# Edge scores by columns sorted on the sign of W2, with self loops as items

## The chip, the cores and the metric

The kernel runs on one core of a Trainium2 chip. The metric is device time in microseconds (us); lower is better. Three runs of the kernel before took 2976.23, 2982.51 and 2991.17 us; the median is 2982.51.

## What is computed

Four graph layers run over 32 batch entries of 512 nodes with 256 features; adj is 512 x 512 and sparse. Layers 0 and 3 are of the kind that this change touches:

```python
pre_u = jnp.einsum('bud,dk->buk', h_t, W1[:d])
pre_v = jnp.einsum('bvd,dk->bvk', h_t, W1[d:])
hidden = jax.nn.relu(pre_u[:, :, None, :] + pre_v[:, None, :, :] + b1)
S = jax.nn.sigmoid(jnp.einsum('buvk,ko->buvo', hidden, W2)[..., 0] + b2[0])
a_t = jnp.einsum('buv,bud->bvd', S * A_a, h_t)
m_t = jnp.einsum('uv,bud->bvd', A_m, h_t) * h_t
z_t = beta1 * h_t + beta2 * (jnp.einsum('bvd,de->bve', a_t, Wa) + ba) \
    + beta3 * (jnp.einsum('bvd,de->bve', m_t, Wm) + bm)
```

Layer 1 is z + relu(adj z W' + b). Layer 2 is a softmax attention whose logits are leaky_relu(f1[i] + f1[j]) + adj. For S the sum over k of relu(pre_u + pre_v + b1) W2 is needed only where adj is not zero, since S is multiplied by adj.

## The kernel before

**Groups and passes.** The batch is worked in eight groups of four entries (NB = 4). For each group and each of layers 0 and 3 there is one pass over the edges, so 16 passes.

**Tables.** `first` (layer 0) and the end of `middle_one` (layer 3) call `pre`. For each entry and each of four chunks of 128 nodes, two matmuls (L592, L594) give pre_u and pre_v; VectorE adds b1 to pre_u (L596), ScalarE copies pre_v (L597), and a DMA on SyncE's queue (SP) writes both as rows to a table in DRAM (L604). Three `puv` buffers take turns. For the self loops `pre` also forms relu(pre_u + b1 + pre_v) (L599) and sums it with W2 into `self_s` (L600).

**Items.** `Edges` holds the edges as 36 items of 128 edges: for each chunk of 128 nodes eight items with one edge a node, and four panels for nodes with more edges. In `edges`, `fetch` loads the pre_u rows of a chunk once as `mine` (L692, SP queue) and for each item gathers pre_v rows by an indirect DMA on GpSimd's queue (POOL). For each item VectorE adds `mine` to `rows` (L731, 1024 elements a partition: four entries by 256 columns). Then one of two ways follows. Every other item has one wide multiply, relu(rows) * W2 (L739), and ScalarE sums the four parts of 256 by activations with an accumulator (L717); the other items have four multiplies of 256 with an accumulator on VectorE (L747). In the first and the last pass (`spare` buffers) ScalarE sums all items. After each four items come an exponential on ScalarE (L614), the rest of the sigmoid on VectorE (L618, L619, L675), and indirect DMAs that put the results into `cells` in DRAM (L639). The self loops have their own sigmoid and two small DMAs to the diagonal (`own_1`).

**The middle stage.** `middle_one` reads `cells` back as SA and runs the rest of layer 0, then layers 1 and 2, and the tables of layer 3, one entry after the other. Its softmax passes between ScalarE (L958, L962), VectorE (L959 to L964) and TensorE transposes (L1003) several times. `last` and, for the last group, `last_before` and `last_behind` do the rest of layer 3 and write the output.

**Order.** `weave` merges these generators by due times given as fractions of a group's middle stage: while group t is in its middle stage, the tables and edges of layer 0 of group t + 1 and the edges and the end of layer 3 of group t - 1 run. `behind` adds an order without a wait, so that an edge operation is not set ahead of the middle stage's last marked operation on that engine. Each engine works its queue in order. The first 245 us hold the preparation: loads, the edge lists (`build`), the tables of groups 0 and 1, and the first edge pass, before the middle stage's own matmuls begin at L891.

Of the kernel before, what the change touches and what calls it, by code (L numbers as in the profile page):

```python
# [16 lines left out]
P = 128  # L17
# [17 lines left out]
EARLY = 20  # L35
CELLS = HALF * N
ITEMS = NC * OWN + 2 * PANELS
SPARE = NC // 2 * OWN * P + LINES
GROUP = NB * D
HELD = 12  # L40

# [7 lines left out]
class Model:  # L49


    def __init__(self, ctx, tc, a):
# [6 lines left out]
        for c in range(NC):  # L59
            nc.sync.dma_start(self.adj[:, c, :], a["adj"][c * P : (c + 1) * P, :])  # L60
        self.g0, self.g3 = self.gnn_first("L0_gnn"), self.gnn_first("L3_gnn")
# [36 lines left out]
    def gnn_first(self, L):  # L98
        nc, a, const = self.nc, self.a, self.const
        w = {"L": L}  # L100
        w["W1"] = self.load(f"{L}_W1", [P, 2 * DC, D], a[f"{L}_W1"].rearrange("(c p) k -> p c k", p=P))
        w["b1bc"] = self.bcast(f"{L}_b1", D)
        w["W2bc"] = const.tile([P, D], F32, name=f"{L}_W2bc")
        nc.scalar.dma_start(w["W2bc"], a[f"{L}_W2"].rearrange("k o -> (k o)").partition_broadcast(P))
        w["b2"] = self.bcast(f"{L}_b2", 1)
        w["nb2"] = const.tile([P, 1], F32, name=f"{L}_nb2")
        w["bcol"] = const.tile([P, DC, 1], F32, name=f"{L}_bcol")
        if L == "L3_gnn":
            w["bbc"] = const.tile([P, D], F32, name=f"{L}_bbc")
# [67 lines left out]
class Counts:  # L177
# [3 lines left out]
    def __init__(self, ctx, m):  # L181
# [4 lines left out]
        with tc.tile_pool(name="c_sb", bufs=2) as sb, tc.tile_pool(name="c_ps", bufs=1, space=PSUM) as ps:  # L186
            ones = sb.tile([P, N], F32, name="c_ones", bufs=1)
            nc.vector.memset(ones, 1.0)
            count = sb.tile([P, NC], F32, name="count", bufs=1)
# [17 lines left out]
            nc.vector.tensor_reduce(half, pc.rearrange("p (h c) -> p h c", h=2), AX.X, ALU.add)  # L207
            most = sb.tile([1, 1], F32, name="most")
            nc.vector.tensor_reduce(most, half, AX.X, ALU.max)
            nc.vector.tensor_scalar(self.excess, most, float(-LINES), None, ALU.add)  # L210
# [193 lines left out]
class Group:  # L404
# [3 lines left out]
    def __init__(self, sp, w, name):  # L408
# [7 lines left out]
        self.self_s = sp.grp.tile([P, NC, NB], F32, name=f"self_s{name[0]}")  # L416

# [5 lines left out]
class Sparse:  # L423
# [3 lines left out]
    def __init__(self, ctx, m, counts, xr, outr, B):  # L427
# [16 lines left out]
        self.act, self.small, self.gath = pool("act", 1), pool("small", 2), pool("gath", 5)  # L444
# [78 lines left out]
    def big(self, dtype, n, layer=None):  # L523

        self.bigs += 1
        if layer is None:
            layer = 3 if self.bigs <= NC else 0
        return self.act.tile([P, n], dtype, name="big", tag=f"SA{layer}", bufs=NC)

    def setup(self):  # L530


        for w in (self.m.g0, self.m.g3):
            self.nc.vector.tensor_scalar(w["nb2"], w["b2"], -1.0, None, ALU.mult)
        self.zero = self.act.tile([P, GROUP], F32, name="zero", tag="hWa3")
# [30 lines left out]
    def setup_rest(self):  # L566
        yield from self.rest

# [13 lines left out]
    def pre(self, g, b, hT):  # L582
# [3 lines left out]
        for c in range(NC):  # L586
            cs = slice(c * P, (c + 1) * P)
            if c % 2 == 0:
# [7 lines left out]
            nc.vector.tensor_tensor(puv[:, 0, :], pp[:, 0:D], w["b1bc"], ALU.add)  # L596
            nc.scalar.copy(puv[:, 1, :], pp[:, D:])  # L597
            both = self.small.tile([P, D], F32, name="both", bufs=1)
            nc.vector.tensor_tensor(both, pp[:, D:], puv[:, 0, :], ALU.add)  # L599
            nc.vector.scalar_tensor_tensor(  # L600
                both, both, 0.0, w["W2bc"], ALU.max, ALU.mult, accum_out=g.self_s[:, c, b : b + 1]
            )
# [47 lines left out]
    def edges(self, g, spare=(), own_tags=()):  # L650
# [8 lines left out]
        tags = [None] * 5 + list(spare)  # L659
# [3 lines left out]
        def own_1():  # L663
            self.sigmoid_of(own)
            diag = self.counts.diag.unsqueeze(2).to_broadcast([P, NC, NB])
            nc.vector.tensor_tensor(g.self_s, g.self_s, diag, ALU.mult)
            for q in range(2):
                diagonal = g.cells[q][q * HALF : q * HALF + HALF * (N + 1), :]
                diagonal = diagonal.rearrange("(c p a) b -> p c a b", p=P, a=N + 1)[:, :, 0, :]
                self.written(g, q, nc.sync.dma_start(diagonal, g.self_s[:, 2 * q : 2 * q + 2, :]))  # L670
# [9 lines left out]
        panels = [j for j in e.order if j >= NC * OWN][: len(own_tags)]  # L680

        def fetch(n):
# [4 lines left out]
            j = e.order[n]  # L687
            c = -j if -j in mine and j >= NC * OWN else j // OWN
# [13 lines left out]
            self.fetch(rows, g, e.iv[:, j : j + 1])  # L702
# [10 lines left out]
        def sums(k, rows):  # L713
# [13 lines left out]
        for k in range(ITEMS):  # L727
# [4 lines left out]
            if k + lead < ITEMS:  # L732
                fetch(k + lead)
# [716 lines left out]
```

## Time and profile before

| | us |
|---|---|
| median of three runs | 2982.51 |
| profiled execution | 2998.45 |
| its span on the core | 2996.8 |

The profiler recorded one execution. Engines are PE (TensorE matmul), PEld (weight load), DVE (VectorE), ACT (ScalarE), POOL (GpSimd) and SP (SyncE). A row of a group gives the line, engine and operation, output and input with their sizes, the count, then the busy time in us and the mean of one in ns, then the idle time of the engine just before them and what ended it. A row of the waits gives who waited for whom, the sum in us, how often and the longest. "issue" is time in which the profile shows no wait. The timeline gives start and duration in us.

The page lists the busy share of PE in 40 slices of 75 us, in tenths: the first eight are 6, 3, 6, 7, 7, 8, 7, 9 and later ones mostly 8 or 9.

### The profile page before, as it was taken

What the parts mean: (1) busy time and instruction counts of PE and PEld (TensorE: products, weight loads), DVE (VectorE), ACT (ScalarE), POOL (GpSimd) and SP (SyncE); (2) the same over time, 40 slices, a digit from 0 to 9 for tenths busy, and PEclk for the clock granted to TensorE, in tenths of its full rate; (3) what the DMA queues carried; (4) which work ended last, traced back from release to release, by engine and by line L of the source; (5) the groups of instructions that cost most, each with busy time, mean ns of one, the idle gap of its engine ahead of it and who ended that gap; (6) DMA issues with size and microseconds to landing.
All of it is one profiled execution on the core that took longest, in us unless ns stands there. A gap on an engine that the chain in (4) does not pass through costs nothing. (4 is left out here: it accounts for less than half of the span.)

```text
span 2996.8 us, 32453 instructions
## 1 busy us (share of the span) xinstructions
PE 2690.0 (90%) x8645; PEld 1613.9 (54%) x8646; DVE 2307.1 (77%) x6035; ACT 1336.8 (45%) x4101; POOL 1555.3 (52%) x1328
## 2 busy tenths in 40 slices
PE   6367787989998999989999899989999899988998
PEld 3134344545664566546664466646565466644666
DVE  6874786889588885988778885888858896783494
ACT  3553454445344443544344443445434453453262
POOL 2662463646445673556536464466735564361183
PEclk9678998999999999999999999999999999999999
DMA  8875657796678867787677866687677866663474
GB/s 268 286 225 169 213 174 221 233 300 203 217 217 269 268 211 227 230 262 254 209 222 247 275 207 230 216 268 253 211 228 236 303 227 197 208 211 102 148 244 150
DMA packets 302143, 677.30 MB, mean 226 GB/s; under 512 B 52608, under 2 KB 170880, under 8 KB 293760
## 3 DMA queue, kind: packets, MB, share of 16 engines
q0 software_dynamic: 122688, 414.40, 42.9%
q1 hardware_dynamic: 160304, 223.52, 23.0%
q10 hardware_dynamic: 18960, 37.24, 3.4%
q8 instruction: 70, 1.15, 0.2%
q14 instruction: 121, 0.99, 0.1%
HBM read 529.02 MB, written 146.01 MB: 225 GB/s over the span
## 5 line engine op out<-in xcount | busy, mean ns | idle before, releaser
L646 POOL DMA_INDIRECT rows<-table,iv x552 | 679.0, 1230 | 795.5 <-DMA table<-puv 262.7
L639 POOL DMA_INDIRECT cells<-s,cell x576 | 697.6, 1211 | 420.6 <-DVE s L675 243.2
L731 DVE TENSOR_TENSOR rows<-rows,mine 128x1024 f32<-128x1024 f32 x552 | 666.4, 1215 | 101.4 <-DMA rows<-table,iv 72.8
L717 ACT ACTIVATE rows<-rows 128x256 f32<-128x256 f32 x1088 | 439.6, 406 | 445.4 <-DVE rows L739 396.6
L46 PE MATMUL pst<-adj,h 128*128 128x512 f32 x1024 | 452.2, 592 | 0.0
L747 DVE SCALAR_TENSOR_TENSOR rows<-rows,L_gnn_W2bc 128x256 f32<-128x256 f32 x1120 | 414.0, 417 | 1.6
L739 DVE SCALAR_TENSOR_TENSOR rows<-rows,L_gnn_W2bc 128x1024 f32<-128x1024 f32 x272 | 329.4, 1213 | 0.4
L46 PEld LDWEIGHTS pst<-adj,h 128*128 128x128 f32 x1024 | 192.8, 190 | 219.9 <-issue 217.6
L46 PE MATMUL pst<-L_gnn_Wa,hT 128*128 128x256 f32 x1024 | 248.8, 393 | 62.9 <-DMA hT<-xT 57.8
L46 PEld LDWEIGHTS pst<-L_gnn_Wa,hT 128*128 128x128 f32 x1024 | 198.9, 199 | 103.0 <-issue 59.2
L46 PE MATMUL pst<-eT,feats 128*128 128x512 f32 x512 | 237.7, 619 | 10.9 <-ACT eT L1004 10.9
L46 PE MATMUL pst<-adjT,zW 128*128 128x512 f32 x512 | 228.2, 599 | 11.6 <-ACT zW L916 9.7
L596 DVE TENSOR_TENSOR puv<-pst,bc_L_gnn_b 128x256 f32<-128x256 f32 x256 | 104.9, 416 | 162.4 <-DMA table<-puv 89.2
L597 ACT COPY puv<-pst 128x256 f32<-128x256 f32 x256 | 93.2, 371 | 288.1 <-DVE puv L596 225.9
L1061 PE MATMUL pst<-hWa,SA 128*128 128x256 f32 x896 | 220.3, 400 | 0.0
L1061 PEld LDWEIGHTS pst<-hWa,SA 128*128 128x128 f32 x896 | 213.8, 328 | 3.7 <-issue 1.7
L717 ACT ACTIVATION_READ_ACCUMULATOR rows<-rows 128x1 f32 x1088 | 204.7, 188 | 0.0
L860 ACT COPY flat<-SA 128x512 f32<-128x512 f32 x128 | 136.7, 1128 | 136.6 <-issue 62.9
L891 PE MATMUL pst<-flat,hWa 128*128 128x512 f32 x448 | 196.8, 592 | 0.0
L592 PE MATMUL pst<-w_L_gnn_W,hT 128*128 128x512 f32 x256 | 141.5, 681 | 53.9 <-ACT hT L579 36.5
L46 PEld LDWEIGHTS pst<-eT,feats 128*128 128x128 f32 x512 | 99.9, 198 | 133.2 <-issue 113.3
L46 PEld LDWEIGHTS pst<-adjT,zW 128*128 128x128 f32 x512 | 96.5, 191 | 133.4 <-issue 114.0
(176 smaller groups left out, 3984.2 us busy)
## 6 DMA issues: line engine op xcount, KB each, us to landing
table<-puv SPq DMA_DIRECT2D x256, 256.0 KB
SA<-cells POOLq DMA_DIRECT2D x64, 1024.0 KB
h<-in_x_dram SPq DMA_DIRECT2D x64, 512.0 KB
mine<-table SPq DMA_DIRECT2D x64, 512.0 KB
hT<-xT SPq DMA_DIRECT2D x36, 512.0 KB
xT<-hT ACTq DMA_DIRECT2D x32, 512.0 KB
x2T<-yT SPq DMA_DIRECT2D x32, 512.0 KB
x2s<-x ACTq DMA_DIRECT2D x64, 256.0 KB
```

What stands on the lines that cost most here:

```text
L46: nc.tensor.matmul(out, lhsT, rhs, start=(n == 0), stop=(n == len(pairs) - 1))
L592: nc.tensor.matmul(pp, hT[:, 0, ks], w["W1"][:, 0::DC, :], start=True, stop=False)
L596: nc.vector.tensor_tensor(puv[:, 0, :], pp[:, 0:D], w["b1bc"], ALU.add)
L639: ins = self.nc.gpsimd.indirect_dma_start(out=g.cells[half], out_offset=bass.IndirectOffsetOnAxis(ap=at, axis=0), in_=s, in_offset=None)
L646: self.nc.gpsimd.indirect_dma_start(out=rows, out_offset=None, in_=g.table, in_offset=bass.IndirectOffsetOnAxis(ap=at, axis=0))
L717: self.behind(nc.scalar.activation(part, part, AF.Identity, accum_out=g.s[:, k, b : b + 1]))
L731: self.behind(nc.vector.tensor_tensor(rows, rows, other, ALU.add))
L739: nc.vector.scalar_tensor_tensor(by_entry, by_entry, 0.0, w2, ALU.max, ALU.mult)
L747: nc.vector.scalar_tensor_tensor(part, part, 0.0, w["W2bc"], ALU.max, ALU.mult, accum_out=at)
L860: self.nc.scalar.copy(flat[:, r, :], SA[r][:, :, b])
L891: nc.tensor.matmul(pz, hWa[:, r, cs], flat[:, r, :], start=(r == 0), stop=False)
L1061: self.nc.tensor.matmul(pz[:, k * D : (k + 1) * D], SA[r][:, cs, b], hWa[:, r, :], start=(r + k == 0), stop=(alone and k == 1 and r == NC ...
```

## The change

- `Counts` gets `ranks`: for each of layers 0 and 3 it counts the positive entries of W2 and gives every column a place: 112 columns (SURE) with positive W2 first, then 112 with negative W2, then the remaining 32 (MIXED). The branch to the dense path is also taken if fewer than 112 columns have one of the signs. W2 and b1 are loaded as columns, not as broadcast rows.
- `sorted_W1` reorders the columns of W1, b1 and W2 with one-hot matrices on TensorE, and scales each of the first 224 columns: pre_u's by -W2 and pre_v's by W2 (su = 1 + sure (-W2 - 1), sv = 1 + sure (W2 - 1)). It runs once for layer 0 in `setup` and once for layer 3 in `setup_rest`. The tables then hold -W2 (pre_u + b1) and W2 pre_v.
- With that, W2 relu(u + v) is max(W2 v, -W2 u) + W2 u for a positive W2 and min(W2 v, -W2 u) + W2 u for a negative one. An item takes a max over 4 x 112 columns, a min over 4 x 112, an add over 4 x 32, and the old multiply over 4 x 32 only. The sum of W2 u over the sure columns depends on the node alone: `pre` forms it with an accumulator (`less`) and it is subtracted from the item's sums; for panels it is subtracted in the rows, over 4 x 224.
- Of every four items ScalarE sums three; VectorE sums the fourth by one reduction over 1024. Self loops become four more items (40 steps a pass): their pre_v rows are loaded by a plain DMA on SP's queue, and ScalarE sums them. `pre` loses the two operations for the self loops.
- `max`, `min` and `add` are set behind the middle stage; before, the add was. The row tiles go from five to six, EARLY from 20 to 24.

```diff
-EARLY = 20
+EARLY = 24
+STEPS = ITEMS + NC
+SURE = 112
+MIXED = D - 2 * SURE
+PLACE = {0: 0, 2: 1, 1: 2, 3: 3}
...
+    def ranks(self, m, sb, ps, ones):
...
+        nc.vector.tensor_scalar(pos, w2, 0.0, None, ALU.is_gt)
+        pb = ps.tile([P, DC, 2], F32, name="c_pb")
+        mm(nc, pb[:, 0, :], [(before, pos[:, 0, :])])
+        mm(nc, pb[:, 1, :], [(before, pos[:, 1, :]), (ones[:, 0:P], pos[:, 0, :])])
+        pn = ps.tile([1, 2], F32, name="c_pn")
+        mm(nc, pn, [(ones[:, 0:1], pos[:, c, :]) for c in range(DC)])
...
+        nc.vector.tensor_scalar(far, rank, float(SURE), float(SURE), ALU.is_ge, ALU.mult)
+        nc.vector.tensor_tensor(place, rank, far, ALU.add)
+        nc.vector.tensor_scalar(far, rank, float(D - SURE), float(SURE - D), ALU.is_ge, ALU.mult)
+        nc.vector.tensor_tensor(place, place, far, ALU.add)
...
+    def sorted_W1(self, w):
...
+        for to, scale in ((by_u, w["su"]), (by_v, w["sv"])):
+            for c in range(DC):
+                nc.vector.tensor_scalar(
+                    to[:, c, :], self.m.upto_D, w["place"][:, c, :], scale[:, c, :], ALU.is_equal, ALU.mult
+                )
+        for c in range(DC):
+            pt = self.psum()
+            for r in range(2 * DC):
+                nc.tensor.transpose(pt[:, r * P : (r + 1) * P], w["W1"][:, r, c * P : (c + 1) * P], self.m.ident)
+            nc.scalar.copy(W1T[:, c, :], pt)
+        for k, to in enumerate((by_u, by_v)):
+            pp = self.psum()
+            for d in range(DC):
+                rs = slice((DC * k + d) * P, (DC * k + d + 1) * P)
+                mm(nc, pp[:, d * D : (d + 1) * D], [(W1T[:, c, rs], to[:, c, :]) for c in range(DC)])
+            nc.scalar.copy(w["W1"][:, DC * k : DC * (k + 1), :], by_two(pp))
...
     def pre(self, g, b, hT):
...
-            nc.vector.tensor_tensor(puv[:, 0, :], pp[:, 0:D], w["b1bc"], ALU.add)
+            nc.vector.scalar_tensor_tensor(
+                puv[:, 0, sure], pp[:, sure], 1.0, w["b1bc"][:, sure], ALU.mult, ALU.add, accum_out=less
+            )
+            nc.vector.tensor_tensor(puv[:, 0, 2 * SURE :], pp[:, 2 * SURE : D], w["b1bc"][:, 2 * SURE :], ALU.add)
             nc.scalar.copy(puv[:, 1, :], pp[:, D:])
-            both = self.small.tile([P, D], F32, name="both", bufs=1)
-            nc.vector.tensor_tensor(both, pp[:, D:], puv[:, 0, :], ALU.add)
-            nc.vector.scalar_tensor_tensor(
-                both, both, 0.0, w["W2bc"], ALU.max, ALU.mult, accum_out=g.self_s[:, c, b : b + 1]
-            )
...
     def edges(self, g, spare=(), own_tags=()):
...
-            self.fetch(rows, g, e.iv[:, j : j + 1])
+            if k < 0:
+                nc.sync.dma_start(rows, places[c, 1])
+            else:
+                self.fetch(rows, g, e.iv[:, j : j + 1])
...
-        todo = [(2, lambda: self.exp_of(w, own)), (4, own_1)]
+        w2 = w["W2bc"].unsqueeze(1).to_broadcast([P, NB, MIXED])
+        todo = [(last_own + 3, own_less), (last_own + 4, own_1)]
...
-            self.behind(nc.vector.tensor_tensor(rows, rows, other, ALU.add))
+            self.behind(nc.vector.tensor_tensor(rows[:, :, ups], rows[:, :, ups], other[:, :, ups], ALU.max))
...
-            if spare or k % 2 == 1 and k < ITEMS - 3:
-                by_entry = rows.rearrange("p (b d) -> p b d", b=NB)
-                w2 = w["W2bc"].unsqueeze(1).to_broadcast([P, NB, D])
-                nc.vector.scalar_tensor_tensor(by_entry, by_entry, 0.0, w2, ALU.max, ALU.mult)
-                summed.append(lambda k=k, rows=rows: sums(k, rows))
+            for cols, op in ((downs, ALU.min), (mixed, ALU.add)):
+                self.behind(nc.vector.tensor_tensor(rows[:, :, cols], rows[:, :, cols], other[:, :, cols], op))
+            nc.vector.scalar_tensor_tensor(rows[:, :, mixed], rows[:, :, mixed], 0.0, w2, ALU.max, ALU.mult)
+            if k >= 0 and e.order[k] >= NC * OWN:
+                sure = slice(0, 2 * SURE)
+                nc.vector.tensor_tensor(rows[:, :, sure], rows[:, :, sure], other[:, :, sure], ALU.subtract)
+            to = g.s[:, k, :] if k >= 0 else g.self_s[:, PLACE[-1 - k], :]
+            if spare or k < 0 or k % 4 and k < ITEMS - 3:
+                line = rows.rearrange("p b d -> p (b d)")
+                summed.append(lambda to=to, line=line: sums(to, line))
                 if spare:
                     summed.pop(0)()
             else:
-                for b in range(NB):
-                    part = rows[:, b * D : (b + 1) * D]
-                    at = g.s[:, k, b : b + 1]
-                    nc.vector.scalar_tensor_tensor(part, part, 0.0, w["W2bc"], ALU.max, ALU.mult, accum_out=at)
+                nc.vector.tensor_reduce(to, rows, AX.X, ALU.add)
...
-    step = (b - a) / ITEMS
+    step = (b - a) / STEPS
```

## The prediction

> **What bounds the kernel now.** The engine sums come first, then the stages, then what ends TensorE's waits in them.
>
> ```profile
> span 2996.8 us, 32453 instructions
> ...
> PE 2690.0 (90%) x8645; PEld 1613.9 (54%) x8646; DVE 2307.1 (77%) x6035; ACT 1336.8 (45%) x4101; POOL 1555.3 (52%) x1328
> ```
>
> TensorE (PE) is the bound, and the change takes nothing from its work. Time can come only out of its 307 us of idle time (2996.8 - 2690.0). The question is where those are. The windows view, cut by stage, has for each stretch the busy time of PE, its weight loads, VectorE (DVE), ScalarE (ACT) and GpSimd (POOL), then the granted TensorE clock, the DMA share and GB/s:
>
> ```profile
> 0.00:90.00 90.00, 57.53 (x193) 31.36 (x194) 54.01 (x199) 32.87 (x84) 26.19 (x44) 0.92 0.85 280
> 90.00:250.00 160.00, 81.30 (x202) 43.87 (x202) 121.60 (x240) 83.92 (x345) 102.35 (x82) 0.73 0.76 251
> 250.00:650.00 400.00, 334.32 (x976) 178.16 (x977) 301.75 (x827) 189.21 (x526) 189.49 (x165) 0.91 0.64 207
> 650.00:2650.00 2000.00, 1906.03 (x6232) 1150.38 (x6230) 1621.83 (x4364) 892.68 (x2674) 1095.39 (x919) 0.99 0.73 235
> 2650.00:2800.00 150.00, 133.02 (x420) 78.64 (x421) 81.89 (x229) 64.41 (x153) 41.93 (x40) 0.94 0.37 121
> 2800.00:2997.00 197.00, 177.76 (x626) 131.53 (x624) 126.03 (x178) 73.72 (x320) 99.96 (x80) 0.96 0.61 203
> ```
>
> PE idles 32, 79, 66, 94, 17 and 19 us in them. So half the idle time lies in the first 650 us. The waits of PE over the whole run, longest first:
>
> ```profile
> PE pst L46 <- DMA hT<-xT: 57.8, 4, 25.7
> PE pst L1003 <- DVE ex L964: 51.7, 27, 10.8
> PE pst L592 <- ACT hT L579: 36.5, 11, 4.9
> PE pst L1003 <- DVE cols L963: 29.3, 8, 6.3
> ```
>
> L1003 is the transposes of the softmax; DVE is late there because it works in order and edge items stand before the softmax. Adding the waits view up stage by stage, waits that DVE ended are 47.2 us in 250 to 650, 58.4 in 650 to 2650 and 22.1 after; those that ACT ended 14.5, 34.1 and 1.5. In 90 to 250 PE waits 57.8 us for hT<-xT: that load needs the buffer which L801, in DVE's queue, still reads.
>
> **The work on DVE.** The groups of the edge stage and of the stage that writes the tables:
>
> ```profile
> L731 DVE TENSOR_TENSOR rows<-rows,mine 128x1024 f32<-128x1024 f32 x552 | 666.4, 1215 | 101.4 <-DMA rows<-table,iv 72.8
> L717 ACT ACTIVATE rows<-rows 128x256 f32<-128x256 f32 x1088 | 439.6, 406 | 445.4 <-DVE rows L739 396.6
> L747 DVE SCALAR_TENSOR_TENSOR rows<-rows,L_gnn_W2bc 128x256 f32<-128x256 f32 x1120 | 414.0, 417 | 1.6
> L739 DVE SCALAR_TENSOR_TENSOR rows<-rows,L_gnn_W2bc 128x1024 f32<-128x1024 f32 x272 | 329.4, 1213 | 0.4
> ```
>
> The means overlap: the timeline of VectorE gives the distance from start to start.
>
> ```profile
> 1401.54 2.35 DVE L731 TENSOR_TENSOR rows<-rows,mine 128x1024 f32<-128x1024 f32 x2
> 1403.82 1.21 DVE L739 SCALAR_TENSOR_TENSOR rows<-rows,L_gnn_W2bc 128x1024 f32<-128x1024 f32 x1
> 1404.95 0.41 DVE L747 SCALAR_TENSOR_TENSOR rows<-rows,L_gnn_W2bc 128x256 f32<-128x256 f32 x1
> 1405.29 0.08 DVE L747 DVE_READ_ACCUMULATOR rows<-rows,L_gnn_W2bc 128x1 f32 x1
> ```
>
> Two operations of 1024 take 2.28 us, one takes 1.14, one of 256 takes 0.345. A line through both is 0.08 us plus 1.035 ns an element: 0.544 for 448 (4x112), 0.212 for 128 (4x32), 1.007 for 896, 0.312 for 224, 0.113 for 32. No row has the strided 4x112 form or max and min; I price them by this line.
>
> Before, over 16 passes of 36 items: 576 adds at 1.14 = 657 us; 296 wide multiplies at 1.14 = 337; 1120 narrow ones at 0.345 = 386; and 768 operations of 256 in `pre` at 0.345 = 265. Together 1645 us.
>
> After, with 40 items a pass, 640 in all: max and min of 448, add and multiply of 128, 1.512 us an item = 968. The 168 items that DVE still sums take one reduction of 1024 each: 168 x 1.14 = 192. The 64 panel items take a subtraction of 896: 64. `pre`: 256 x (0.312 + 0.113) = 109. Subtracting `less`, about 160 operations of 16 elements at 0.09 (neighbour: L618): 14. Together 1347. **DVE loses 298 us**, 18.6 a pass.
>
> [...]
>
> **The work on ACT.** Items summed there go from 296 to 472: 704 more activations. In the timeline ACT starts one every 0.40 us with its accumulator read, so +282 us, 45% to 54% of the span. [...] The rows agree on price, 4 x 0.40 = 1.60 us an item on ACT against 1.14 for a reduction on DVE: 176 items cost 81 us of engine time more. [...] I decide by whose queue PE waits for: DVE is 81% busy in the long stage, ACT 45%.
>
> **Stage by stage, against the 2998.45 us of the profiled execution.**
>
> 0 to 90: **+1**. Ahead of the branch some 20 small operations join the chain behind the last mask (neighbours 0.08 to 0.20 us apart): +3. Behind it the first layer's sort is 8 transposes, 12 matmuls and 4 ACT copies of 0.58, before the first matmul with W1 at 24.8; h arrives at 21, so about 2 of it shows. `pre` of the first group gives back 16 x 0.61 = 9.8 on DVE, of which I credit 4, as DVE waits 12.5 there for table<-puv. Bounds -3 to +8. The second layer's sort, PE work of some 4 us, falls where PE idles.
>
> 90 to 250: **-15**. DVE is packed from 90 to 182. 36 x 2.28 becomes 40 x 1.51 + 4 x 1.01: -17.6; `pre` of the second group -9.8; second sort +2. Of these 25 I credit 60%, as DVE also waited 38 us here. ACT's four more items (6.4 us) fit into its 76 idle us. Bounds 0 and -25.
>
> 650 to 2650: **-19**. ACT sums 744 / 4 = 186 items here, so some 11.6 passes: DVE -216, from 81% to 70% busy. If waiting behind other work goes with busy over idle, 4.3 becomes 2.4: 45% off the 58.4 us, -26. ACT goes to 56% by the same count (139 items x 1.60 = 223); that alone would add 56% to its 34.1 us, +19. But ACT is held up too: "ACT rows L717 <- DVE rows L739" is 299 us here and ACT's five longest waits for DVE make 624; shorter ones there give the 223 back. Between 0 and +19 I take +7. Bounds -50 and +25.
>
> 250 to 650: **-18**: 45% of 47.2 less 3 for ACT. No clock gain is credited. Bounds -45 and +10.
>
> 2650 to the end: **-9**, 45% of 22.1 less 1. The last pass sums all on ACT, 64 us instead of 58, beside DVE's 36 x 2.28 = 82 that becomes 65; the 28 us of L1061 behind the SA loads stay. Bounds 0 and -20.
>
> **Costed at nothing.** POOL keeps its 576 row fetches and 576 puts. The 64 loads of own rows, 512 KB each, go into SP's queue in order, where each waits for one of six row buffers; behind it stand table<-puv, h, hT and x2T. SP's mine loads, the nearest case, wait 6.6 us each ("SPq L692 <- DVE rows L731: 146.0, 22, 16.3"), yet after 650 PE waits only 0.8 us for any load in the long stage. If that slack is gone, 64 x 6.6 us of queue time is what can leak. The diagonal's sigmoid moves from step 4 to about step 28 of 40; its two small writes still stand ahead of the last puts.
>
> **Sum**: 1 - 15 - 18 - 19 - 9 = -60: 2998.45 becomes 2938. The median of the runs, 2982.51, is 0.9947 of the profiled execution; so **2923 us**.
>
> **Rivals.**
> 1. *ACT takes DVE's place, slower.* Place: the middle stage's copies (hT, zW, eT), queued in order behind a sum that waits for DVE. For it: 115 of the 186 summed items waited, 2.6 us each. If waits do not shorten, 326 items give 202 waits, 525 us blocked, and ACT is (893 + 624 + 223 + 226) / 2000 = 98% taken. One more such wait on the path in each of 32 batch entries is +83 us, against the gains of 60: 3021, by the median 3005. It decides from 60 / 32 = 1.9 us an entry. Against it: an item's DVE part falls from 2.28 to 1.51 us.
> 2. *Transfers hide the gain.* In 650 to 2650 DVE waits 64.7 us for table<-puv and 46.4 for rows, with DMA at 0.73, and 64 x 512 KB = 33.6 MB come on top of 677 MB. Then only start and end gain: 1 - 15 - 9, and about +5 for the transfers: -18, 2980, by the median 2965. Against it: PE's DVE waits end mostly with softmax operations.
> 3. *More is freed.* Idle between 90 and 2800 falls by nearly half (-120) as stalls chain, and the clock of 0.91 before 650 recovers: 2878, by the median 2863.
> 4. The branch could choose the dense path if a sign count left 112 to 144; both layers' W2 have 133 positive of 256. Nothing is reserved for it.
>
> **Chances**: forecast 0.50, rival 1 0.17, rival 2 0.20, rival 3 0.13. A measurement here tells 0.5% from no change, 2967.6 to 2997.4. Faster: nearly all of the forecast and of rival 3 and under half of rival 2, 0.70; same 0.15; slower 0.15. The range 2850 to 2988 leaves out most of rival 1 and the low end of rival 3.
>
> **What would show it.** Right: DVE near 2010 us, ACT near 1620, POOL unchanged; the waits on L964 and L963 halved; the first softmax transposes before 272 us instead of 282. Wrong: waits of PE on ACT copies over 100 us (rival 1); DVE's waits on rows and table<-puv grown by what its work lost (rival 2); 4x112 operations over 0.62 us apart.

## The result, and the profile after

Four runs of the changed kernel took 3020.24 to 3036.07 us, median **3031.07**; four of the kernel before 2976.23 to 2991.17, median 2985.21. The ratio is **1.0152** (95% interval 1.0126 to 1.0177): the change made the kernel 45 us slower, where 60 us less was forecast. The profiled execution took 3036.07 us; that of the kernel before, 2998.45, was slower than each of its four runs here.

The page's head and its first row, the busy time of each engine:

```profile
span 3034.4 us, 34147 instructions
...
PE 2708.6 (89%) x8720; PEld 1631.4 (54%) x8720; DVE 1994.7 (66%) x5677; ACT 1612.4 (53%) x5517; POOL 1401.9 (46%) x1332
```

VectorE lost 312 us of work and ScalarE gained 276, near the 298 and 282 worked out. TensorE's idle time, which was to shrink by 60, went from 307 to 326 us. The windows view of the changed kernel, cut as before (columns: us of the stretch, then busy time of PE, PEld, DVE, ACT and POOL, granted clock, DMA share, GB/s):

```profile
0.00:90.00 90.00, 61.72 (x228) 35.87 (x228) 60.10 (x258) 38.83 (x101) 23.76 (x44) 0.98 0.79 256
90.00:250.00 160.00, 85.64 (x243) 50.48 (x244) 87.56 (x295) 88.13 (x368) 87.65 (x85) 0.75 0.84 290
250.00:650.00 400.00, 342.08 (x1013) 183.02 (x1012) 270.58 (x767) 232.73 (x753) 177.37 (x171) 0.92 0.71 227
650.00:2650.00 2000.00, 1896.05 (x6177) 1147.25 (x6176) 1388.76 (x3862) 1098.14 (x3745) 979.12 (x909) 0.98 0.75 244
2650.00:2800.00 150.00, 124.69 (x366) 68.83 (x365) 72.14 (x197) 64.52 (x179) 45.30 (x44) 0.91 0.41 130
2800.00:3034.00 234.00, 198.46 (x699) 145.90 (x697) 115.54 (x302) 90.01 (x373) 88.66 (x80) 0.93 0.54 183
```

Idle time of PE by stage is now 28, 74, 58, 104, 25 and 36 us, where it was 32, 79, 66, 94, 17 and 19: less up to 650 us, more behind it. A second measure does not depend on fixed cuts: the time at which ScalarE makes the second yT copy (L922 before, L1061 after) of each of the 32 entries. The fifth comes at 508.9 us before and 491.5 after, 17 us earlier. Half of that can be scatter: in e4 below, VectorE runs the same first 475 operations as in the kernel before, and the 469th of them starts at 274.2 us there and at 282.6 here. The 29th comes at 2581.0 and 2590.9, so the stretch between them, the long stage from here on, lost 27. From the 29th to the end it is 415.8 and 443.5: another 28 lost.

For this long stage the time splits into three parts: idle time of PE, what the low clock costs (an estimate: half of PE's busy time in the stretches that the clock record shows at 0.5, as a 128x512 matmul of the changed kernel starts 0.85 us after the one before it there and 0.43 at full clock), and a rest that differs by 8 us at most. Each row is one profiled execution; the last four are experiments told below.

| kernel | stretch | PE idle | low clock | rest |
|---|---|---|---|---|
| before | 2072.0 | 112.4 | 25.3 | 1934.3 |
| after | 2099.4 | 125.9 | 40.5 | 1933.0 |
| no self loops (e2) | 1985.5 | 49.6 | 9.4 | 1926.5 |
| their loads only (e6) | 2022.7 | 70.9 | 22.7 | 1929.1 |
| their items, no loads (e7) | 2067.1 | 108.3 | 31.1 | 1927.7 |
| self loops in `pre` (e15) | 2032.2 | 80.1 | 18.6 | 1933.5 |

So the 27 us are 13.5 more of idle time and 15 more of low clock. The waits view, TensorE's waits over the whole run (sum in us, times, longest), with rows left out where dots stand:

```profile
PE pst L51 <- DMA hT<-xT: 46.1, 3, 16.1
PE pst L1142 <- DVE cols L1102: 44.4, 7, 8.6
PE pst L684 <- DVE yT L1120: 34.5, 6, 7.2
PE pst L682 <- ACT hT L669: 30.5, 15, 4.6
PE pst L1212 <- DVE big L940: 18.5, 4, 14.6
...
PE pst L684 <- ACT hT L669: 13.4, 6, 3.2
...
PE pst L1142 <- DVE ex L1103: 9.3, 14, 0.7
```

The softmax waits on ex did fall, from 51.7 us (L964) to 9.3 (L1103). In their place stands a wait that was hardly there before (8.0 us in six waits at L592 and L594): **L684, six times, some 6 us each**, once in six of the eight groups. L684 is the second half of the layer-3 table products; it needs the second half of x2T, which VectorE makes at L1120. The timeline of VectorE in one group:

```profile
1658.47 0.74 DVE L1120 SCALAR_TENSOR_TENSOR yT<-pst,col_L_gnn_bias,yT 128x512 f32<-128x512 f32 x1
...
1659.33 0.16 DVE L708 TENSOR_SCALAR s<-s 128x8 f32<-128x8 f32 x1
1664.44 0.62 DVE L862 TENSOR_TENSOR rows<-rows,mine 128x448 f32<-128x448 f32 x1 [4.95 <-issue]
1664.98 1.21 DVE L880 TENSOR_REDUCE s<-rows 128x4 f32<-128x1024 f32 x1
...
1669.34 0.74 DVE L1120 SCALAR_TENSOR_TENSOR yT<-pst,col_L_gnn_bias,yT 128x512 f32<-128x512 f32 x1
```

The two halves of x2T are 10.9 us apart, with 13 edge operations in between. One of them, a maximum, waits 4.95 us. The view finds no releaser ("issue"). TensorE's product for the second half (L51) ends at 1661.4; VectorE, idle from 1659.5 to 1664.44, still comes to L1120 only at 1669.34, behind the edge operations in its queue. Each of the six stalls follows a wait of VectorE at L862 like this one, of 4.6 to 6.2 us; two of the six end with the landing of rows<-table,iv, and in e1 and e7 below all six do. Why are those rows late? The timeline of GpSimd just before:

```profile
1648.48 0.94 POOL L736 DMA_INDIRECT mine<-table,iu  x1 [14.57 <-DVE rows L872]
1650.45 1.13 POOL L729 DMA_INDIRECT cells<-s,cell  x1 [1.03 <-DVE s L792]
...
1657.22 0.99 POOL L736 DMA_INDIRECT rows<-table,iv  x1 [0.30 <-issue]
```

GpSimd stood 14.57 us before a panel's first-row tile, until L872, the panels' new subtraction, had read the old one; then five puts (L729) went ahead of the row fetch. GpSimd's waits have this, too, six times:

```profile
POOL mine L736 <- DVE rows L872: 78.5, 6, 14.6
```

Each of the six, 11 to 15 us long, ends some 22 to 24 us before one of the six stalls ends. What a stall of that length does to TensorE is read from windows of 4 us around it (columns as above):

```profile
1660.00:1664.00 4.00, 4.00 (x11) 1.84 (x10) 0.00 (x0) 2.52 (x3) 3.08 (x4) 1.00 1.00 299
1664.00:1668.00 4.00, 1.04 (x4) 0.28 (x2) 3.56 (x8) 1.63 (x2) 1.89 (x3) 1.00 0.59 221
1668.00:1672.00 4.00, 1.86 (x2) 0.84 (x3) 3.56 (x9) 0.59 (x2) 3.07 (x4) 0.59 0.69 160
1672.00:1676.00 4.00, 4.00 (x7) 1.67 (x6) 3.75 (x15) 0.37 (x1) 2.49 (x4) 0.55 0.98 347
```

The timeline of TensorE has the matmuls on both sides of it:

```profile
1661.22 3.60 PE L682 MATMUL pst<-w_L_gnn_W,yT 128*128 128x512 f32 x8
...
1670.13 6.38 PE L684 MATMUL pst<-w_L_gnn_W,yT 128*128 128x512 f32 x8 [5.10 <-DVE yT L1120]
```

PE is idle from 1665.0 to 1670.1; the clock is at 0.5 from 1668.7 to 1675.6. The eight matmuls after the stall take from 1670.13 to the start of the next at 1676.35, 6.2 us; the eight at full clock before it (L682) take 3.4, 0.43 each. So a stall of 5.1 us costs 7.9.

At the end of the run the longest single wait is on `DVE big L940` (14.6 us). VectorE's timeline shows the same picture, an operation that TensorE needs behind edge items in the queue, which wait for rows:

```profile
2937.13 0.62 DVE L862 TENSOR_TENSOR rows<-rows,mine 128x448 f32<-128x448 f32 x1 [5.12 <-DMA rows<-table,iv]
...
2940.62 0.63 DVE L862 TENSOR_TENSOR rows_more<-rows_more,mine_more 128x448 f32<-128x448 f32 x1 [1.93 <-DMA rows_more<-table,iv]
...
2943.93 0.68 DVE L940 TENSOR_TENSOR big<-pst,hT 128x512 f32<-128x512 f32 x1
```

### The profile page after: what moved, and what is told of

Its sections match the earlier page's. It is cut to its first block, busy times and chain, and to the rows that moved or that the text cites. A ratio compares the mean times of both kernels' runs of the same rounds, so it can differ in the third digit from the quotient of the medians.

```text
span 3034.4 us, 34147 instructions
## 1 busy us (share of the span) xinstructions
PE 2708.6 (89%) x8720; PEld 1631.4 (54%) x8720; DVE 1994.7 (66%) x5677; ACT 1612.4 (53%) x5517; POOL 1401.9 (46%) x1332
## 4 chain that ended last, share of the span: by engine, by line
PE 50%; DVE 19%; DMA 15%; issue 8%; ACT 5%; POOL 2%; SPq 0%; ACTq 0%; another core or an unknown queue 0%; POOLq 0%; DVEq 0%
PE pst L51 21%; DMA rows<-table,iv 6%; DMA table<-puv 5%; PE pst L1200 5%; PE pst L684 5%; PE pst L682 5%; DVE rows L868 4%; PE pst L1030 4%; DVE rows L862 3%; PE pst L1051 2%; ACT rows L846 2%; PE pst L1212 2%; PE pst L1073 2%; DVE s L880 2%; PE pst L1037 2%
## 5 line engine op out<-in xcount | busy, mean ns | idle before, releaser
L736 POOL DMA_INDIRECT rows<-table,iv x558 | 624.5, 1119 | 927.6 <-ACT rows L846 280.6
L846 ACT ACTIVATE rows<-rows 128x256 f32<-128x256 f32 x1792 | 722.4, 406 | 343.1 <-DVE rows L869 255.5
L729 POOL DMA_INDIRECT cells<-s,cell x576 | 621.0, 1078 | 265.4 <-issue 138.3
L868 DVE TENSOR_TENSOR rows<-rows,mine 128x448 f32<-128x448 f32 x1232 | 513.2, 444 | 0.0
L862 DVE TENSOR_TENSOR rows<-rows,mine 128x448 f32<-128x448 f32 x616 | 379.8, 617 | 172.7 <-DMA rows<-table,iv 135.4
L51 PE MATMUL pst<-adj,h 128*128 128x512 f32 x1024 | 452.8, 593 | 4.5 <-ACT puv L692 4.5
L846 ACT ACTIVATION_READ_ACCUMULATOR rows<-rows 128x1 f32 x1792 | 338.6, 189 | 8.0 <-issue 7.7
L51 PEld LDWEIGHTS pst<-adj,h 128*128 128x128 f32 x1024 | 192.8, 190 | 225.8 <-issue 216.7
L51 PE MATMUL pst<-L_gnn_Wa,hT 128*128 128x256 f32 x1024 | 249.6, 394 | 52.2 <-DMA hT<-xT 46.1
L688 DVE SCALAR_TENSOR_TENSOR puv<-pst,L_gnn_b1bc 128x224 f32<-128x224 f32 x256 | 99.0, 387 | 285.5 <-DMA table<-puv 134.1
L51 PE MATMUL pst<-eT,feats 128*128 128x512 f32 x512 | 230.8, 604 | 23.1 <-ACT eT L1143 13.3
L51 PEld LDWEIGHTS pst<-L_gnn_Wa,hT 128*128 128x128 f32 x1024 | 199.3, 199 | 92.3 <-issue 61.8
L51 PE MATMUL pst<-adjT,zW 128*128 128x512 f32 x512 | 231.0, 605 | 7.8 <-issue 4.4
L880 DVE TENSOR_REDUCE s<-rows 128x4 f32<-128x1024 f32 x168 | 203.2, 1210 | 1.0
L999 ACT COPY flat<-SA 128x512 f32<-128x512 f32 x128 | 134.4, 1116 | 112.4 <-PE pst L51 87.1
L682 PE MATMUL pst<-w_L_gnn_W,hT 128*128 128x512 f32 x256 | 136.5, 660 | 52.0 <-ACT hT L669 30.5
L869 DVE SCALAR_TENSOR_TENSOR rows<-rows,L_gnn_W2bc 128x128 f32<-128x128 f32 x616 | 174.8, 285 | 3.8 <-remote 1.1
L51 PEld LDWEIGHTS pst<-eT,feats 128*128 128x128 f32 x512 | 96.6, 192 | 143.3 <-issue 111.1
```

The source lines that it names most:

```text
L51: nc.tensor.matmul(out, lhsT, rhs, start=(n == 0), stop=(n == len(pairs) - 1))
L682: nc.tensor.matmul(pp, hT[:, 0, ks], w["W1"][:, 0::DC, :], start=True, stop=False)
L729: ins = self.nc.gpsimd.indirect_dma_start(out=g.cells[half], out_offset=bass.IndirectOffsetOnAxis(ap=at, axis=0), in_=s, in_offset=None)
L736: self.nc.gpsimd.indirect_dma_start(out=rows, out_offset=None, in_=g.table, in_offset=bass.IndirectOffsetOnAxis(ap=at, axis=0))
L846: self.behind(nc.scalar.activation(part, part, AF.Identity, accum_out=to[:, b : b + 1]))
L862: self.behind(nc.vector.tensor_tensor(rows[:, :, ups], rows[:, :, ups], other[:, :, ups], ALU.max))
```

## The experiments

Each ratio is to the kernel before on the same chip, with its 95% interval; differences in us are differences of ratios times the kernel before. e2, e6 and e14 take the sorted kernel without its self-loop items, and e8, e13 and e15 to e17 put the self loops back into `pre`; with that EARLY is 20 again in all of these, and in e13 and e15 to e17 one constant is held in bf16. The theories: **A**, ScalarE's added sums make the copies late that TensorE needs; **B**, the self loops as items (their loads: queue, B1, or bytes, B2; or their place and time in the queues, B3); **C**, the order of an item's pieces.

### What sorting is worth, and what the self loops cost

**e2: without the self-loop items** (the diagonal of S is left out; EARLY is 20).

```diff
-STEPS = ITEMS + NC
+STEPS = ITEMS
...
-                seq.append(-1 - c)
...
-            self.behind(nc.vector.tensor_tensor(own, own, g.less.rearrange(flat), ALU.subtract))
+            self.behind(nc.vector.tensor_scalar(own, g.less.rearrange(flat), 0.0, None, ALU.mult))
```

> The changed kernel without its 64 self-loop items: no own-row loads (33.6 MB), no operations on them, the diagonal is left out of what is computed. Theory B (the loads in SyncE's queue and their bytes): 30 us or more off, to 3000 or less, and VectorE's waits for rows and for the tables' buffers come back to 73 and 89 us from 135 and 134. Theory A: 256 activations less, a third of what was added: some 10 to 15 us off. Theory C: under 10 us.

Measured: **0.9755** (0.9734 to 0.9776), 4.0% or 118 us below the changed kernel. B holds in its first half, far beyond its number. Against the kernel before this one is 73 us faster. But VectorE's waits for rows and table buffers did not come back to 73 and 89 us:

```profile
DVE puv L688 <- DMA table<-puv: 139.7, 46, 8.8
DVE rows L861 <- DMA rows<-table,iv: 115.1, 71, 11.8
```

With 255 us of such waits this kernel is the fastest of all, so their growth, from 162 to 270 us in the changed kernel, is not by itself what makes that one slow. Of the 135 us between the two profiles, 114 lie in the long stage (2099.4 less 1985.5): 76 of idle time and 31 of low clock. Of the idle time 38 are waits that VectorE ended, 34.5 of them the stalls at L684, and 33 waits that ScalarE ended.

**e9: the kernel before without its self loops** (the diagonal is left out).

```diff
-            nc.vector.tensor_tensor(both, pp[:, D:], puv[:, 0, :], ALU.add)
-            nc.vector.scalar_tensor_tensor(
-                both, both, 0.0, w["W2bc"], ALU.max, ALU.mult, accum_out=g.self_s[:, c, b : b + 1]
-            )
```

> The kernel before without its two self-loop operations in the stage that writes the tables (512 operations of 256 elements, 177 us of VectorE); the diagonal is left out. With it the four corners are there: sorted or not, self loops or not. If sorting alone is worth what the run without self-loop items showed (ratio 0.9755) and the old self loops cost little on the path, this is 0.99 or more; if the old self loops cost as much on the path as the 64 new items (some 120 us), it is 0.965 or less and sorting gives nothing; between the two, the share of each is read from it.

Measured: **0.9979** (0.9965 to 0.9993). Its page has

```profile
PE 2689.0 (91%) x8646; PEld 1617.3 (55%) x8646; DVE 2127.4 (72%) x5283; ACT 1337.4 (45%) x4101; POOL 1566.9 (53%) x1328
```

VectorE has 180 us less to do than before, and the time falls by 6 us. It waits more instead, for rows 124 us where it was 73:

```profile
DVE rows L730 <- DMA rows<-table,iv: 123.7, 62, 8.3
```

**e6: the loads without the items** (e2 and, for each chunk, an own-row load on SP's queue into a row tile that nothing reads).

```diff
+            if 0 <= c < NC and c not in lone:
+                lone.add(c)
+                spare_rows = self.gath.tile([P, GROUP], F32, name="rows")
+                nc.sync.dma_start(spare_rows, places[c, 1])
```

> The run without self-loop items (ratio 0.9755), with the 64 own-row loads put back into SyncE's queue, each into a row buffer that nothing reads: bytes, queue and buffer are there, the operations on them are not; the diagonal is left out. Theories B1 and B2: most of the way back, 1.00 or more. Theory B3: 0.985 or less.

Measured: 0.9893 (0.9875 to 0.9912), 1.4% above e2: some 41 us for the loads, each with a row tile of its own. It lies between the two expectations.

**e7: the items without the loads** (an item reads the first-row tile twice, so the diagonal is wrong).

```diff
-            if k < 0:
-                nc.sync.dma_start(rows, places[c, 1])
...
+            read = rows if k >= 0 else other
```

> The changed kernel with the 64 self-loop items, but without their own-row loads: their three operations read the tile of the first rows twice, so the diagonal is not the reference's. All of VectorE's and ScalarE's work is there. Theories B1 and B2: near the run without self loops, 0.985 or less. Theory B3: 1.00 or more.

Measured: 1.0047 (1.0033 to 1.0062): 2.9% above e2, 87 us for the items, and 1.05% below the changed kernel, 31 us for the loads. B3 is the larger part: 87 us for the items and 31 to 41 for the loads. The waits of TensorE at the table products tell them apart. e7, with items:

```profile
PE pst L684 <- DVE yT L1119: 36.6, 6, 6.8
```

e6, with loads alone:

```profile
PE pst L682 <- DVE yT L1123: 4.9, 6, 1.5
```

The six stalls of 6 us appear in each run that has self-loop items in the pass and six row tiles (after, e1, e5, e7, e11, e12, e18: 32 to 37 us, five or six times) and in none with sorted columns that has no such items (e2, e6, e8 and e13 to e17); nor has GpSimd the six long waits for L872 in e2, e6 and e15. So the four more steps a pass bring the stalls, by what they put between the two halves of x2T. They are not all: e1 and e7 keep them and are 35 and 31 us faster than the changed kernel.

**e5: own rows from GpSimd's queue.**

```diff
-                nc.sync.dma_start(rows, places[c, 1])
+                nc.gpsimd.dma_start(rows, places[c, 1])
```

> The changed kernel with the 64 own-row loads issued from GpSimd's queue, where the fetched rows come from too, instead of SyncE's. Theory B1 (SyncE's queue: what stands behind a load that waits for a row buffer is late): 40 us or more off the 1.0152 of the changed kernel, to a ratio of 1.002 or less. Theory B2 (the bytes) or B3 (the place and time of 64 more items in VectorE's and ScalarE's queues): within 0.5% of 1.0152, or worse, as GpSimd's own fetches then wait behind these.

Measured: 1.0126 (1.0105 to 1.0146). The interval overlaps that of the changed kernel, and the 40 us that B1 asked for are not there. SP's queue is at most a small part of what the loads cost, unless GpSimd's queue costs as much in its place.

**e14: no self loops, five row tiles** (e2 with 6 made 5 in the pool and in `tags`).

> The run without self-loop items (0.9755) with five row tiles instead of six; the diagonal is left out. If what made it fast is the spare row tile that the self loops' steps would take, it goes back to 0.99 or more; if it is VectorE's smaller work, it stays below 0.982.

Measured: 0.9861 (0.9845 to 0.9877), between the two. Against e9, also without self loops and with five tiles, sorting and the new shares are worth 1.2% (35 us); the sixth tile gives 1.1% more (32 us). With the 6 us of the old self loops these make up the 73 us of e2.

### ScalarE's share

**e1: half the sums.**

```diff
-            if spare or k < 0 or k % 4 and k < ITEMS - 3:
+            if spare or k % 2 == 1 and 0 < k < ITEMS - 3:
```

> The changed kernel (3031 us), with ScalarE summing every second item as before and the self loops' items summed on VectorE: 704 of the added activations go (282 us of ScalarE), VectorE gets 176 reductions more (200 us). If ScalarE's longer queue is what makes TensorE late (theory A): TensorE's waits for the copies of h (hT, 30 + 13 us) fall to about the 36 us of before and the time falls by 20 us or more, to 3010 or less. If the own-row loads and transfers are the cause (theory B) or the order of the pieces of an item (theory C): within 8 us of 3031, or slower, as VectorE is fuller.

Measured: 1.0035 (1.0022 to 1.0047), 1.2% or 35 us less than the changed kernel. The time fits A, the waits less well:

```profile
PE pst L682 <- ACT hT L669: 52.9, 18, 14.8
...
PE pst L684 <- DVE yT L1120: 33.1, 6, 6.2
...
PE pst L684 <- ACT hT L669: 3.5, 2, 2.4
```

The second wait for hT fell from 13.4 to 3.5, the first grew from 30.5 to 52.9 (one of 14.8 us), and the stalls for yT stayed.

**e4: three of four sums in the kernel before.**

```diff
-            if spare or k % 2 == 1 and k < ITEMS - 3:
+            if spare or k % 4 and k < ITEMS - 3:
```

> The kernel before with one edit: ScalarE sums three of four items. 448 activations more (+180 us on ScalarE), VectorE loses 112 x 4 small multiplies but takes 112 wide ones (about -155 + 128 = -27 us). Theory A: slower than 2985 by 15 us or more. Theories B and C: within 8 us of 2985.

Measured: 1.0082 (1.0065 to 1.0099), 24 us slower, as A expected.

**e11: the changed kernel, half the sums in the first and last pass only.**

```diff
-            if spare or k < 0 or k % 4 and k < ITEMS - 3:
+            if (n % 2 if spare else k < 0 or k % 4 and k < ITEMS - 3):
```

> The changed kernel with only the first and last pass edited: there ScalarE sums every second step instead of all 40. If ScalarE is what makes the end late (443 us from the 29th batch entry's yT to the end, 416 before), the end takes 430 us or less and the ratio is 1.010 or less; if it is the order in VectorE's queue, 440 us or more and 1.013 or more.

Measured: 1.0089 (1.0065 to 1.0114); the end takes 428.9 us instead of 443.5. So about 19 us of the loss (0.6%, each interval 0.25% to either side) come from ScalarE summing all 40 steps of a pass at the two ends.

**e18: only the self-loop items' sums back on VectorE.**

```diff
-            if spare or k < 0 or k % 4 and k < ITEMS - 3:
+            if spare or k > 0 and k % 4 and k < ITEMS - 3:
```

> The changed kernel with one edit: outside the first and last pass the self-loop items are summed on VectorE, the others as in the change (three of four on ScalarE). ScalarE loses 56 x 4 activations (90 us), VectorE gains 56 reductions (64 us). If the self-loop items' sums are what half the sums (1.0035) cured, the ratio is 1.007 or less; if it was the share of the ordinary items, 1.012 or more.

Measured: **1.0237** (1.0202 to 1.0273), on the side of the ordinary items' share (1.012 or more), but slower than the changed kernel, which neither side foresaw. Taking 90 us off ScalarE made it worse, where taking 282 off (e1) made it better. In its profile the long stage has 143.3 us of idle time and 47.7 of low clock.

### The order

**e3: only the maximum behind the middle stage.**

```diff
-    self.behind(nc.vector.tensor_tensor(rows[:, :, cols], rows[:, :, cols], other[:, :, cols], op))
+    nc.vector.tensor_tensor(rows[:, :, cols], rows[:, :, cols], other[:, :, cols], op)
```

> The changed kernel with only the first operation of an item (the maximum) held behind the middle stage, as only the add was before; minimum, add and multiply may go where the scheduler likes. Theory C (order): TensorE's stalls of 5 to 7 us before the second half of the table products (waiting for yT) go, 15 us or more off 3031. Theories A and B: within 8 us.

Measured: **1.1436** (1.1411 to 1.1460), the reverse of what C expected. The minimum and the add read other columns than the maximum. Without the order VectorE comes to them (L868) before their rows are there:

```profile
DVE rows L868 <- DMA rows<-table,iv: 609.4, 220, 15.4
```

In the changed kernel that line waits for no rows. So the order put on all three keeps the cut items from costing 13% more.

**e10: half the sums, four first-row tiles and five row tiles.**

```diff
-        self.act, self.small, self.gath = pool("act", 1), pool("small", 2), pool("gath", 6)
+        self.act, self.small, self.gath = pool("act", 1), pool("small", 2), pool("gath", 5)
...
-                t = self.gath.tile([P, GROUP], F32, name="mine", bufs=3)
+                t = self.gath.tile([P, GROUP], F32, name="mine", bufs=4)
```

> The run with half the sums (ratio 1.0035) with four tiles for first rows and five for second rows instead of three and six. GpSimd's fetch of a panel's first rows then waits no longer for the subtraction of the panel three tiles before. If that wait is what makes the rows late between the two halves of x2T (TensorE's 6 stalls of 5 to 6 us for yT), these stalls go, and 30 to 45 us with their clock: ratio 0.992 or less. If the row tiles are what is short, it is 1.0035 or more.

Measured: 1.0271 (1.0248 to 1.0294). GpSimd's waits for a panel's tile on L872 are gone from the view (82.6 us in e1), and the stalls at L684 fall from 33.1 to 21.9 us, the longest from 6.2 to 4.2: the chain over the panel's tile is part of them. The two edits were not run apart; VectorE's waits for rows are 164 us instead of 110, which fits the row tile that is missing.

### Versions

**e8, e13: self loops back in `pre`, half the sums, with five and with six row tiles.** The self loops take the maximum, minimum, add and multiply on the two halves of `puv`, and one activation sums them:

```diff
+            for cols, op in ((ups, ALU.max), (downs, ALU.min), (mixed, ALU.add)):
+                nc.vector.tensor_tensor(both[:, cols], puv[:, 1, cols], puv[:, 0, cols], op)
+            nc.vector.scalar_tensor_tensor(both[:, mixed], both[:, mixed], 0.0, w["W2bc"], ALU.max, ALU.mult)
+            nc.scalar.activation(both, both, AF.Identity, accum_out=to)
```

> Sorted columns, but the self loops as before in the stage that writes the tables, on the two halves that lie in fast memory there (four operations of 112, 112, 32 and 32 elements on VectorE, 0.65 us, and one summing activation on ScalarE, for each of 256 pieces), five row tiles, ScalarE summing every second item: no own-row loads, no self-loop items. VectorE has 256 x 0.65 - 64 x 1.51 = 70 us more than with items, or about 2240. If the self-loop items are what costs (theory B, either form), the ratio is below 0.995, faster than both kernels; if the time goes with VectorE's busy time, it is 1.00 or more.

> The run with self loops in the stage that writes the tables (ratio 1.0088 with five row tiles), with six row tiles. If the sixth tile is worth what half the sums showed for one tile less (1.0035 to 1.0271), this is 0.99 or less. If self loops cost by their work on VectorE and ScalarE, wherever it is done, it stays at 1.005 or more.

Measured: 1.0088 (1.0054 to 1.0122) and 1.0053 (1.0032 to 1.0073): no gain over e1 (1.0035), and the tile is not told apart here. This speaks against B, which expected less than 0.995 of e8: at half the sums, self loops cost as much in `pre`, with ScalarE summing them, as they do as items that VectorE sums.

**e15: the same with three of four sums, six tiles**: the change with the self-loop items taken back, and EARLY with them.

> Sorted columns, ScalarE sums three of four items as in the change, six row tiles, self loops in the stage that writes the tables: the change with only the self-loop items taken back. The run without self loops is at 0.9755 and the old self loops cost 0.2% of the time in the kernel before. If self loops as steps of the pass (a row tile, a load, a place in the order) are what costs, this is 0.985 or less, 45 us faster than the kernel before; if their work on VectorE and ScalarE is, 0.995 or more.

Measured: **0.9944** (0.9927 to 0.9962), faster than both kernels, by 2.0% than the changed one. It lies between the two bounds, near the upper one, and 1.9% above e2. So of the 118 us, 62 go when the self loops are no steps of the pass, and 56 stay with them in `pre`. Why they cost 56 there, when in the kernel before they cost 6 in the same place, is open; e17 shows that it is not ScalarE's sums alone. Set beside e13, three of four is here the better share by 1.1%, where in the changed kernel half was better by 1.2%. The gain of 62 us is thus one for three of four sums; at half it is none.

**e16: e15 with half the sums in the first and last pass** (e11's edit).

> As the run before it, with ScalarE summing every second item in the first and last pass, which took 0.6% off the changed kernel. If the end is late for ScalarE there too, 0.3 to 0.6% less than the run before it; if the end was late only because of the self-loop steps, no difference beyond 0.2%.

Measured: **0.9926** (0.9910 to 0.9943), the fastest that leaves nothing out; it is not told apart from e15, so its question stays open.

**e12: half the sums, also at the ends, and own rows from GpSimd** (the edits of e1, e11 and e5).

> The parts that helped, together: half the sums on ScalarE, in the first and last pass too, and own rows from GpSimd's queue. If their effects add (1.0035 less 0.0026 for the queue and some 0.003 for the end), the ratio is about 0.998; faster than the kernel before only if the end gives more.

Measured: 1.0041 (1.0018 to 1.0064). The parts do not add to the 0.998 expected: with e1 alone it was 1.0035.

**e17: e16 with the self loops' sums on VectorE's accumulators.**

```diff
-            nc.scalar.activation(both, both, AF.Identity, accum_out=to)
+                nc.vector.scalar_tensor_tensor(
+                    both[:, :SURE], puv[:, 1, cols], 1.0, puv[:, 0, cols], ALU.mult, op, accum_out=to[:, k : k + 1]
+                )
...
+                nc.vector.tensor_reduce(g.self_s[:, :, b : b + 1].rearrange("p c o -> p (c o)"), parts, AX.X, ALU.add)
```

> The fastest version so far (ratio 0.9926) with the self loops' sums taken by VectorE's own accumulators instead of 256 activations: ScalarE loses 256 x 0.40 = 102 us and its 111 us of waits for these operands, VectorE gains three accumulator reads and a share of a small reduction for each of 256 pieces, some 60 us. If ScalarE's order is what still holds the copies of h back (44 us of TensorE's waits), the ratio falls to 0.988 or less; if VectorE's work decides, it rises to 0.995 or more.

Measured: 1.0044 (1.0023 to 1.0065), 1.2% slower than e16, the side on which VectorE's work decides.

## Why the prediction was wrong

**Right: the work.** VectorE ended at 1994.7 us (forecast near 2010), ScalarE at 1612.4 (near 1620). The 4x112 operations last 0.62 us, but the next starts after 0.54 (1664.44 to 1664.98 above), as the line through the old rows gave; after a reduction of 1024, priced at 1.14, the next starts after 1.13. GpSimd, which was to stay as it was, shows 1401.9 us for 1555.3, with four instructions more.

**In number near: the start.** By the fifth entry it was 17 us earlier; the forecast had 1 - 15 and some part of the -18 up to there. This is one pair of profiles, half of the 17 can be scatter, and the sign named for it failed: the first softmax transposes came at 278.5 us, not before 272. The profile of e9 reaches the fifth entry at 486.0 without sorting, so the gain is not shown to be the sort's.

**Right in kind: sorting frees TensorE.** Without the self-loop items the kernel is 73 us faster than before (e2), but this does not bear out the 60 of the sum: 32 of the 73 come with the sixth row tile, for which the sum had no term, and 6 with the old self loops. Sorting and the new shares gave 35. The waits on ex fell as foretold; those on cols did not (29.3 before, 44.4 after).

**The step that failed: self loops priced as busy time.** The sum put the old self loops into VectorE's "768 operations of 256 in `pre`" and the new ones into the 640 items, and let one amount stand against the other: 298 us less, of which a share would show. By e9 the old ones were worth 6 us, not the 180 us of their busy time; by e2 the new ones cost 118 us. 118 less 73 is, as it must be, the 45 us by which the kernel became slower. Each new item is a step in a pass that works in order: it takes a row tile, shifts what stands between two operations that TensorE waits for (the stalls at L684), and stands in the last pass (end 443.5 us, 424.7 in e2). Taking the items back to `pre` gave 62 of the 118 us (e15). But the place alone does not set the price: 56 us stayed there, and with half the sums on ScalarE the move gave nothing (e1 against e13). How the items and ScalarE's share act together is open.

**"Costed at nothing": the 64 own-row loads.** They cost 31 us (after less e7) to 41 (e6 less e2). The bound given for this, 64 x 6.6 us of queue time, named SP's queue: from another queue they cost about as much (e5, 1.0126 for 1.0152). In the 31 the row tile as such is not, as e7's items take one too. The load's bytes and its longer hold on the tile were not told apart.

**650 to 2650, "45% off": waits in proportion to busy over idle.** This was the author's estimate, and no run shows it: waits of TensorE that VectorE ended fell from 67.9 to 57.9 us between the fifth and the 29th entry, by only 15%, since the stalls at L684 came in. Those that ScalarE ended rose from 39.2 to 62.5, by 23 instead of 7. And the low clock, which the sum left out, took 15 more than before.

**2650 to the end, "-9".** It was +28 from the 29th entry on. In the last pass ScalarE's 64 us of sums, beside 65 us of VectorE's, were held to be free; e11 shows about 19 us for the sums of the first and last pass.

**The rivals.** Rival 1 had the side right (3005 for 3031), and e1 and e4 show that more sums on ScalarE can cost 24 to 35 us. Its sign, over 100 us of waits on ScalarE's copies, was not reached: 78 us in the whole run, 63 before. Its place was half right: in the long stage the waits for hT rose from 24.0 to 36.6 and those for eT from 4.1 to 8.3, but those for zW fell from 8.3 to 2.9. And e18, e13 and e15 show the sign of ScalarE's share changing with the rest of the order. So ScalarE is not the cause by itself, and why these small moves go either way by 1% is open. Rival 2's sign was there in part: VectorE's waits for rows and tables grew by 108 us, not by the 312 that its work lost, and by e2 they are no cause by themselves.

## What to carry to other kernels

Do not price moved work by how long it is: taking 180 us of VectorE's work out of the kernel before gave 6 us, and four more steps in each pass of the sorted kernel, with less of VectorE's work, cost 118. Before an engine's relief is turned into time, look at which operation that the bound engine waits for stands behind which transfer in that engine's queue, and test the change in halves: here one half was worth -2.4% and the other +4.0%. Give a spare buffer its own run: the sixth tile was almost half of the gain. When shares between two engines are tuned, do it last, for the best share turned round with the order.

## What the runs showed of the hardware

The clock records of the two kernels, before and after, hold two values, 1.0 and 0.5, and their steps lie 3.41 us or a multiple of it apart. In the 3.41 us before each of the 72 falls to 0.5 (34 before, 38 after) TensorE was busy 0 to 1.70 us (by the profile's times, in which the ends of matmuls are modelled): in 22 of them not at all, in the other 50 part of the time. Before 46 of the 72 no idle stretch that reached into these 3.41 us was, up to the fall, as long as they are. In the 1527 other such stretches of the record at full clock, after which it did not fall, TensorE was busy 1.50 us or more, and in those before the 70 rises 2.77 us or more. These are counts from two profiles; no run was made to find what sets the clock.

At 0.5 a 128x512 matmul of the changed kernel starts 0.85 us after the one before it (median of 20), at full clock 0.43 (median of 2003). So its stalls cost more than their own length: 7.9 us for the one of 5.1 us above, and in the long stage 40 us of low clock beside 126 us of idle time.
